# Four fused graph layers on Trainium2: the adjacency checks move to the input buffers, two chunks' operand pairs move to the last stage's buffers, and one subtraction moves from GpSimd to VectorE

## The chip, the cores and the metric

The kernel runs on one core of a Trainium2 chip. A core has a matrix engine (TensorE, "PE" in the profile), a vector engine (VectorE, "DVE"), a scalar engine (ScalarE, "ACT"), a general engine (GpSimd, "POOL") and a sync engine ("SP") that issues transfers between device memory (HBM) and the on-chip memory SBUF. PE writes its results into a second on-chip memory, PSUM. The metric is the device time of one execution in microseconds (us). A lower time is better. In the profile, "PEld" is PE loading the stationary operand of a matmul, and "PEclk" is the clock that PE was granted, as a share of full speed.

## The reference, cut to what matters

Four layers follow one another, each of the form x = x + layer(relu(layernorm(x))), on x of 8 batches x 2048 nodes x 64 features, with a 2048 x 2048 adjacency of zeros and ones. The change lies in the code of layers 2 and 3 only:

```python
# layer 2: three steps
v = causal_vars.at[:, intervention_idx].set(intervention_value)
for _ in range(3):
    effects = einsum('nm,bmd->bnd', adj, v)
    h = relu(einsum('bnk,dk->bnd', concatenate([v, effects], -1), W1) + b1)
    v = einsum('bnk,dk->bnd', h, W2) + b2
# layer 3: Chebyshev terms of the adjacency, then node-wise weights
w = einsum('nd,dkio->nkio', embedding, weight)          # d = 16, k = 3
x_g = stack([x, A @ x, 2 * A @ (A @ x) - x])            # over k
out = einsum('bnki,nkio->bno', x_g, w) + embedding @ bias
```

So for each batch there are five products with the adjacency: three in layer 2 and two in layer 3.

## The kernel before, in words

**Layout.** Two batches are handled as a pair p (of four): 2 x 64 features lie on the 128 partitions, the 2048 nodes along the free axis, in four chunks c of 512 columns. The transposed adjacency stays in SBUF as 16 tiles of 128 rows (`aT`, the last four named `aTl` in the profile).

**The product with the adjacency.** `spread` (L1459) adds up 16 row tiles into one PSUM tile `acc` per chunk. For precision each operand is two float32r tiles, `hi` (the rounded value) and `lo` (what the rounding left), so a chunk takes 32 matmuls. The operand pairs of the four chunks are made by `moved` (L1431), from matmuls with a small weight into PSUM (`py`), or by `turned` (L1448), from transposes. In `moved` with a bias, VectorE writes `yb` (L1443), ScalarE rounds it to `hi` (L1444) and GpSimd subtracts to get `lo` (L1445). In the other cases VectorE makes `lo` (L1440 and L1456).

**Stages of one pair.** `enter` (L1468) loads a chunk of the pair's input (`xp`), normalises it with `norm` (PE `mean`, DVE `xc`, ACT `q`, PE `var`, ACT, DVE `v`; L719 to L727) and makes the first operand pair. Then three steps follow, each over four chunks: step 0 and 1 make the next step's operands with `moved` (`yb` of chunk c belongs to the next step). Step 2 adds the input again (`xq`), writes the sum with a bias (`bq`) to device memory, normalises and makes operands with `turned`. Then one more product (`y1`), and the last stage: a product per chunk (`y2`), and for each of its four node tiles k a transpose (`px`), twelve matmuls `u` (L1541), products with the embedding (`pr`, L1549), their sums (L1553), a first addition into `fold` (L1559) and, on GpSimd, the rest (L1560 to L1562) and the store of `ot`. In the last stage of pair p the chunks of pair p+1 are entered; the last one, c = 3, after the loop, so that it meets the last tile's operations and the start of the next step 0.

**The checks.** The fused code holds only if the adjacency is zeros and ones. `check` (L1410) loads a 128 x 512 piece of it (`raw`, L1417, on SP's queue) and has VectorE compare it in place (L1419), with the number of offenders in a column of `bad`. There are 64 pieces. `check(2)` is called for every chunk of every step, so the first pair and the second take 24 checks each and the third 16. After everything, a flag made from `bad` decides on a slower general path, which this input doesn't take.

**Buffers and order.** A tile takes the next buffer of its tag in a pool; with n buffers it waits for the readers of the tile n earlier. Pool `f_in` has two buffers for tag "x" (`xp` of `enter`, `xq` of step 2, `xr` of the last stage). Pool `f_sb` has tags "hi" and "lo" with six buffers each, "fold" with two and "pr" with three (`pr` and `bq`). `raw` is in "fold". Each engine executes its own list of instructions in order, and SP issues its transfers in order. A scheduler sets these lists when the program is built; they can differ from the order of the source.

Of the kernel before, what the change touches and what calls it, by code (L numbers as in the profile page):

```python
# [8 lines left out]
FP = mybir.dt.float32  # L9
FR = mybir.dt.float32r  # L10
AF = mybir.ActivationFunctionType
OP = mybir.AluOpType
# [4 lines left out]
P = 128  # L17
# [4 lines left out]
CW = 512  # L22
# [5 lines left out]
def half(b2):  # L28
    return slice(b2 * 64, (b2 + 1) * 64)


def cols(c, w=CW):
    return slice(c * w, (c + 1) * w)
# [1353 lines left out]
def layers23(kit, aT, x2_dram, x3_dram, out):  # L1387

    tc, nc, t = kit.tc, kit.nc, kit.t
# [3 lines left out]
    W1v, W1e, W2, Wvc, Wec, cb = kit.W1v, kit.W1e, kit.W2, kit.Wvc, kit.Wec, kit.cb  # L1393
# [3 lines left out]
    fin = ctx.enter_context(tc.tile_pool(name="f_in", bufs=2, reuse_waits="tile"))  # L1397
    w2 = ctx.enter_context(tc.tile_pool(name="w2f", bufs=1, reuse_waits="tile"))
    sb = ctx.enter_context(tc.tile_pool(name="f_sb", bufs=2, reuse_waits="tile"))
    ps = ctx.enter_context(tc.tile_pool(name="f_ps", bufs=2, space=PSUM, reuse_waits="tile"))  # L1400

    def norm(dst, src):

        mean = ps.tile([P, CW], FP, tag="tp", name="mean")
        var = ps.tile([P, CW], FP, tag="tp", name="var")
        xc = fin.tile([P, CW], FP, tag="ca", name="xc")
        q = fin.tile([P, CW], FP, tag="q", name="q", bufs=1)
        kit.norm(dst, src, mean, var, xc, q)

    def check(n):  # L1410

        for _ in range(n):
            if not todo:
                return
            m, h = todo.pop(0)
            a = sb.tile([P, CW], FP, tag="fold", name="raw")
            nc.sync.dma_start(out=a, in_=t["adjT"][m * P : (m + 1) * P, cols(h)])  # L1417
            k = 7 + NCW * m + h
            nc.vector.scalar_tensor_tensor(  # L1419
                a, a, 0.5, a, op0=OP.is_gt, op1=OP.not_equal, accum_out=kit.bad[:, k : k + 1]  # L1420
            )

    todo = [(m, h) for m in range(NT) for h in range(NCW)]

    def parts():
        return (
            sb.tile([P, 4, P], FR, tag="hi", name="hi", bufs=6),
            sb.tile([P, 4, P], FR, tag="lo", name="lo", bufs=6),
        )

    def moved(v, c, W, bias):  # L1431

        py = ps.tile([P, 4, P], FP, tag="tp", name="py")
        for k in range(4):
            m = 4 * c + k
            mm(py[:, k, :], v[:, m * P : (m + 1) * P], W, start=True, stop=True)  # L1436
        hi, lo = parts()
        if bias is None:
            nc.scalar.copy(hi, py)
            nc.vector.tensor_tensor(lo, py, hi.bitcast(FP), op=OP.subtract)  # L1440
        else:
            yb = fin.tile([P, 4, P], FP, tag="ca", name="yb")
            nc.vector.tensor_tensor(yb, py, bias[:, None, :].to_broadcast([P, 4, P]), op=OP.add)  # L1443
            nc.scalar.copy(hi, yb)  # L1444
            nc.gpsimd.tensor_tensor(lo, yb, hi.bitcast(FP), op=OP.subtract)  # L1445
        return hi, lo

    def turned(v, c):  # L1448

        tp = ps.tile([P, 4, P], FP, tag="tp", name="tp")  # L1450
        for k in range(4):
            m = 4 * c + k
            nc.tensor.transpose(tp[:, k, :], v[:, m * P : (m + 1) * P], ident)
        hi, lo = parts()
        nc.scalar.copy(hi, tp)  # L1455
        nc.vector.tensor_tensor(lo, tp, hi.bitcast(FP), op=OP.subtract)  # L1456
        return hi, lo

    def spread(acc, y, c, start):  # L1459

        for m in range(NT):
            for part in y[m // 4]:
                mm(acc, part[:, m % 4, :], aT[m][:, cols(c)], start=start, stop=m == NT - 1 and part is y[m // 4][1])  # L1463
                start = False

    v = fin.tile([P, N], FP, name="v", bufs=1)
# [19 lines left out]
    for p in range(NP):  # L1486
        for step in range(3):
            yn = []
            for c in range(NCW):
                acc = ps.tile([P, CW], FP, tag="acc", name="acc")  # L1490
                check(2)
                mm(acc, Wvc if step else W1v, v[:, cols(c)], start=True, stop=False)  # L1492
                spread(acc, y, c, False)
                nc.scalar.activation(v[:, cols(c)], acc, AF.Relu, bias=b1c if step else b1)
                if step < 2:
                    yn.append(moved(v, c, Wec, cb))
                    continue
                pv = ps.tile([P, CW], FP, tag="tp", name="pv")
                mm(pv, W2, v[:, cols(c)], start=True, stop=True)
                xp = fin.tile([P, CW], FP, tag="x", name="xq")  # L1500
                nc.sync.dma_start(out=xp, in_=x2_dram[p, :, cols(c)])
                nc.vector.scalar_tensor_tensor(xp, pv, b2c, xp, op0=OP.add, op1=OP.add)
                bq = sb.tile([P, CW], FP, tag="pr", name="bq", bufs=3)
                nc.sync.dma_start(out=bq, in_=kit.bias_dram[:, cols(c)])
                nc.gpsimd.tensor_add(bq, bq, xp)
                nc.sync.dma_start(out=x3_dram[p, :, cols(c)], in_=bq)
                norm(v[:, cols(c)], xp)
                yn.append(turned(v, c))
            y = yn


        y1 = sb.tile([P, N], FP, tag="y1", name="y1", bufs=1)
        yn, after = [], []
        for c in range(NCW):
            acc = ps.tile([P, CW], FP, tag="acc", name="acc")
            spread(acc, y, c, True)
            nc.scalar.copy(y1[:, cols(c)], acc)
            yn.append(turned(y1, c))
        for c in range(NCW):
            acc = ps.tile([P, CW], FP, tag="acc", name="acc")  # L1520
            spread(acc, yn, c, True)
            y2 = fin.tile([P, CW], FP, tag="ca", name="y2")
            nc.scalar.copy(y2, acc)
            xp = fin.tile([P, CW], FP, tag="x", name="xr")
            nc.sync.dma_start(out=xp, in_=x3_dram[p, :, cols(c)])
            if c > 0 and p + 1 < NP:
                after.append(enter(p + 1, c - 1))
            for k in range(4):
                i = 4 * c + k
                ns, ks = slice(i * P, (i + 1) * P), slice(k * P, (k + 1) * P)  # L1530
                px = ps.tile([P, P], FP, tag="tp", name="px")
                nc.tensor.transpose(px, xp[:, ks], ident)
                xs = sb.tile([P, 2, F], FP, tag="xs", name="xs", bufs=1)
                nc.scalar.copy(xs.rearrange("p h f -> p (h f)"), px)
                pr = []
                for w in range(2):
                    u = [ps.tile([P, 8, F], FP, tag=f"u{h}", name=f"u{h}") for h in range(2)]
                    for kk, src in enumerate((v[:, ns], y1[:, ns], y2[:, ks])):
                        for h in range(2):

                            one = mm(  # L1541
                                u[h].rearrange("p d o -> p (d o)"), src[half(h), :], W3[half(h), kk, cols(w)],
                                start=kk == 0, stop=kk == 2,
                            )
                            if kk or h:
                                tc.keep_in_program_order(one)
                    for h in range(2):
                        a = sb.tile([P, 8, F], FP, tag="pr", name="pr", bufs=3)
                        nc.vector.tensor_tensor(  # L1549
                            a, u[h], emb[:, i, 8 * w : 8 * w + 8, None].to_broadcast([P, 8, F]), op=OP.mult  # L1550
                        )
                        if w:
                            nc.vector.tensor_add(pr[h], pr[h], a)  # L1553
                        else:
                            pr.append(a)
                fold = sb.tile([P, 2, 4, F], FP, tag="fold", name="fold")
                ot = sb.tile([P, 2, F], FP, tag="ot", name="ot", bufs=1)
                for h in range(2):
                    nc.vector.tensor_add(fold[:, h], pr[h][:, 0:4, :], pr[h][:, 4:8, :])  # L1559
                nc.gpsimd.tensor_add(fold[:, :, 0:2, :], fold[:, :, 0:2, :], fold[:, :, 2:4, :])  # L1560
                nc.gpsimd.tensor_add(ot, fold[:, :, 0, :], fold[:, :, 1, :])  # L1561
                nc.gpsimd.tensor_add(ot, ot, xs)  # L1562
                nc.sync.dma_start(
                    out=out[2 * p : 2 * p + 2, ns, :].rearrange("h p f -> p h f"), in_=ot
                )
        y = after + [enter(p + 1, NCW - 1)] if p + 1 < NP else None
# [102 lines left out]
```

## Time and profile before

| | |
|---|---|
| three runs | 2201.65, 2203.05, 2203.95 us; median 2203.05 us |
| the profiled execution | 2206.68 us, its span 2204.9 us |
| mean granted clock of PE | 0.98 |
| PE busy | 2091.0 us (95%), 9132 matmuls |
| VectorE busy | 1220.0 us (55%) |
| ScalarE busy | 450.4 us (20%) |
| GpSimd busy | 299.3 us (14%) |
| layers 2 and 3 | about 1014 us to the end, some 297 us per pair |
| in 1010 to 2205 us | PE busy 1161.0, VectorE 458.2, ScalarE 177.0, GpSimd 169.2 us |
| chain that ended last | PE 54%, issue 23%, DMA 7%, DVE 6%, POOL 5% of the span |

A line of the groups reads: source line, engine, operation, output <- inputs, their shapes and types, count, then busy time in us and mean ns of one, then the idle time of the engine just before such instructions and what ended it. A line of the timeline has its start in us, its duration, the instruction and, in brackets, the idle time before it and what ended that. A line of the waits has the waiting instruction, the instruction it waited for, the total in us, the number of waits and the longest. Busy times on PE are those of the records, whose ends are modelled and overlap; the pace is read from one start to the next. "PEld" overlaps PE.

### The profile page before, as it was taken

How to read it: one execution, taken by the hardware profiler on the slowest of the kernel's cores; microseconds unless marked ns; L12 is line 12 of the kernel's file. 1: busy time of each engine (PE TensorE's matmuls, PEld its weight loads, DVE VectorE, ACT ScalarE, POOL GpSimd, SP SyncE). 2: the span in 40 equal slices, each digit the busy share in tenths (PEclk: the TensorE clock that was granted, in tenths of full speed). 3: DMA queues.
4: the chain of work that ended last, by engine and by line, in shares of the span. 5: the costliest groups of instructions: out<-in, count | busy, mean ns of one | idle time of the engine just before them, and what ended most of it. 6: DMA issues, size and time to landing. Idle time of an engine off the chain costs nothing.

```text
span 2204.9 us, 23720 instructions
## 1 busy us (share of the span) xinstructions
PE 2091.0 (95%) x9132; PEld 1153.5 (52%) x9132; DVE 1220.0 (55%) x1890; ACT 450.4 (20%) x848; POOL 299.3 (14%) x416
## 2 busy tenths in 40 slices
PE   7999899886999999998999998999999999999997
PEld 4776656522222222224766546774457664576653
DVE  6675588866878787884213564115551235501265
ACT  4322244464110202002121101120111201112100
POOL 0211154401000000000110121101111011211022
PEclk9999899998999999999999999999999999999999
DMA  4665362156011111104210014000130100101000
GB/s 122 195 205 153 102 216 50 37 157 194 19 58 34 44 39 53 39 29 122 77 43 8 22 26 133 21 23 16 28 93 13 44 10 21 42 1 34 11 18 12
DMA packets 86443, 141.32 MB, mean 64 GB/s; under 512 B 33072, under 2 KB 33328, under 8 KB 84080
## 3 DMA queue, kind: packets, MB, share of 16 engines
q1 hardware_dynamic: 68272, 89.10, 13.7%
q0 software_dynamic: 18048, 50.60, 7.6%
q8 instruction: 74, 1.21, 0.2%
q14 instruction: 49, 0.40, 0.1%
HBM read 108.93 MB, written 30.74 MB: 63 GB/s over the span
## 4 chain that ended last, share of the span: by engine, by line
PE 54%; issue 23%; DMA 7%; DVE 6%; POOL 5%; ACT 2%; SPq 0%; POOLq 0%; DVEq 0%; ACTq 0%
PE acc L1463 16%; PE o L1332 11%; PE dn L1338 6%; PE u L1541 4%; DMA raw<-in_adjT 3%; PE acc L913 3%; PE pgs L1136 2%; PE var L724 2%; POOL fold L1560 2%; PE mean L719 2%; PE py L1436 1%; PE acc L1492 1%; DVE ex L1134 1%; POOL ot L1561 1%; POOL ot L1562 1%
## 5 line engine op out<-in xcount | busy, mean ns | idle before, releaser
L1463 PE MATMUL acc<-aT,hi 128*128 128x512 f32 x960 | 401.4, 418 | 0.0
L1463 PE MATMUL acc<-aT,lo 128*128 128x512 f32 x960 | 388.5, 405 | 0.0
L1332 PE MATMUL o<-pt,hS 128*64 128x512 f32 x1024 | 268.2, 606 | 4.3 <-DVE pt L1347 4.3
L1347 DVE SCALAR_TENSOR_TENSOR pt<-R,wd,aT 128x1024 f32<-128x1024 f32 x192 | 238.9, 1280 | 41.5 <-PE dn L1338 20.8
L1541 PE MATMUL u<-W3f,y 64*128 64x512 f32 x1024 | 258.2, 592 | 0.0
L1549 DVE TENSOR_TENSOR pr<-u,embf 128x512 f32<-128x512 f32 x256 | 171.3, 687 | 123.1 <-PE u L1541 111.0
L1463 PEld LDWEIGHTS acc<-aT,hi 128*128 128x128 f32 x960 | 180.9, 188 | 61.8 <-issue 23.2
L1463 PEld LDWEIGHTS acc<-aT,lo 128*128 128x128 f32 x960 | 180.9, 188 | 51.4 <-issue 13.6
L1541 PEld LDWEIGHTS u<-W3f,y 64*128 64x128 f32 x1024 | 104.1, 187 | 124.8 <-issue 124.8
L1332 PEld LDWEIGHTS o<-pt,hS 128*64 128x64 f32 x1024 | 70.5, 137 | 185.9 <-issue 178.7
L1541 PE MATMUL u<-W3f,v 64*128 64x512 f32 x512 | 146.4, 617 | 0.0
L1338 PE MATMUL dn<-pt,vd 128*32 128x512 f32 x1024 | 143.8, 600 | 0.5 <-DVE pt L1347 0.5
L913 PE MATMUL acc<-at,Y 128*128 128x512 f32 x512 | 139.2, 419 | 1.8 <-DVE ev L922 1.8
L1463 PE MATMUL acc<-aTl,lo 128*128 128x512 f32 x320 | 129.1, 404 | 5.5 <-DVE lo L1440 3.7
L1463 PE MATMUL acc<-aTl,hi 128*128 128x512 f32 x320 | 128.2, 401 | 6.0 <-ACT hi L1444 6.0
L1560 POOL TENSOR_TENSOR fold<-fold 128x256 f32<-128x256 f32 x64 | 47.6, 744 | 555.9 <-DVE fold L1559 555.9
L913 PEld LDWEIGHTS acc<-at,Y 128*128 128x128 f32 x512 | 97.5, 198 | 25.2 <-issue 3.4
L1443 DVE TENSOR_TENSOR yb<-py,cb_f 128x512 f32<-128x512 f32 x32 | 22.1, 690 | 158.4 <-PE py L1436 158.4
L721 ACT ACTIVATE q<-xc 128x512 f32<-128x512 f32 (+1 forms) x56 | 38.7, 691 | 262.7 <-DVE xc L720 256.0
L1553 DVE TENSOR_TENSOR pr<-pr 128x512 f32<-128x512 f32 x128 | 88.1, 688 | 2.2
L1419 DVE SCALAR_TENSOR_TENSOR raw<-raw 128x512 f32<-128x512 f32 x64 | 48.3, 760 | 72.5 <-DMA raw<-in_adjT 72.5
L1456 DVE TENSOR_TENSOR lo<-tp,hi 128x512 fp32r<-128x512 f32 x32 | 22.1, 692 | 117.5 <-ACT hi L1455 117.5
(275 smaller groups left out, 2694.9 us busy)
## 6 DMA issues: line engine op xcount, KB each, us to landing
at<-in_adjT POOLq DMA_DIRECT2D x32, 512.0 KB, 4.6
raw<-in_adjT SPq DMA_DIRECT2D x64, 256.0 KB, 3.3
aT<-in_adjT POOLq DMA_DIRECT2D x12, 1024.0 KB, 6.6
R<-r_dram SPq DMA_DIRECT2D x16, 512.0 KB, 3.6
hi_dram<-hi SPq DMA_DIRECT2D x16, 264.0 KB, 2.5
lo_dram<-lo SPq DMA_DIRECT2D x16, 264.0 KB, 3.4
hhi<-hi_dram POOLq DMA_DIRECT2D x16, 264.0 KB, 3.1
hlo<-lo_dram POOLq DMA_DIRECT2D x16, 264.0 KB, 3.2
```

What stands on the lines that cost most here:

```text
L719: mm(mean[:, cols(c)], self.avg, src[:, cols(c)], start=True, stop=True)
L724: mm(var[:, cols(c)], self.avg, q[:, cols(c)], start=True, stop=True)
L913: mm(acc[p], Y[h][:, m, p, :], at[:, k, :], start=m + h == 0, stop=m == NT - 1 and h == 1)
L1332: mm(o[half(b2), cols(k)], hS[:, m, half(b2)], pts[b2][:, cols(k)], start=m == 0, stop=m == NT - 1)
L1338: mm(dn[q : q + 32, :], vd[:, m, b2 : b2 + 1].to_broadcast([P, 32]), pts[b2][:, cols(k)], start=m == 0, stop=m == NT - 1, tile_position=(0 ...
L1347: nc.vector.scalar_tensor_tensor(pt, R[b2], wd[:, m, b2 : b2 + 1], aT[m][:, s].bitcast(FP), op0=OP.max, op1=OP.mult)
L1419: nc.vector.scalar_tensor_tensor(a, a, 0.5, a, op0=OP.is_gt, op1=OP.not_equal, accum_out=kit.bad[:, k : k + 1])
L1463: mm(acc, part[:, m % 4, :], aT[m][:, cols(c)], start=start, stop=m == NT - 1 and part is y[m // 4][1])
L1541: one = mm(u[h].rearrange("p d o -> p (d o)"), src[half(h), :], W3[half(h), kk, cols(w)], start=kk == 0, stop=kk == 2,)
L1549: nc.vector.tensor_tensor(a, u[h], emb[:, i, 8 * w : 8 * w + 8, None].to_broadcast([P, 8, F]), op=OP.mult)
L1553: nc.vector.tensor_add(pr[h], pr[h], a)
L1560: nc.gpsimd.tensor_add(fold[:, :, 0:2, :], fold[:, :, 0:2, :], fold[:, :, 2:4, :])
```

## The change

It has four parts, all in `layers23`. First, a check's tile `raw` takes a buffer of tag "x" in `f_in` and not of "fold" in `f_sb`. Second, `check(2)` is called in steps 0 and 1 only, so that each of the four pairs has 16 checks. Third, the operand pairs of chunks 2 and 3 that are made in steps 0 and 2 take their `hi` and `lo` from tags "fold" (chunk 2) and "pr" (chunk 3). Fourth, `lo` of `moved` with a bias is made on VectorE and not on GpSimd. In the changed file the lines up to L1425 keep their numbers and later ones stand 5 or 6 further on (L1443 to L1445 become L1448 to L1450).

```diff
     def check(n):
...
-            a = sb.tile([P, CW], FP, tag="fold", name="raw")
+            a = fin.tile([P, CW], FP, tag="x", name="raw")
             nc.sync.dma_start(out=a, in_=t["adjT"][m * P : (m + 1) * P, cols(h)])
...
-    def parts():
+    def parts(lent=None):
+
+        if lent:
+            return tuple(sb.tile([P, 4, P], FR, tag=lent[0], name=n, bufs=lent[1]) for n in ("hi", "lo"))
         return (
             sb.tile([P, 4, P], FR, tag="hi", name="hi", bufs=6),
             sb.tile([P, 4, P], FR, tag="lo", name="lo", bufs=6),
         )
 
-    def moved(v, c, W, bias):
+    LENT = (None, None, ("fold", 2), ("pr", 3))
+
+    def moved(v, c, W, bias, lent=None):
...
-        hi, lo = parts()
+        hi, lo = parts(lent)
...
             nc.scalar.copy(hi, yb)
-            nc.gpsimd.tensor_tensor(lo, yb, hi.bitcast(FP), op=OP.subtract)
+            nc.vector.tensor_tensor(lo, yb, hi.bitcast(FP), op=OP.subtract)
...
-    def turned(v, c):
+    def turned(v, c, lent=None):
...
-        hi, lo = parts()
+        hi, lo = parts(lent)
...
-                check(2)
+                if step < 2:
+                    check(2)
...
                 if step < 2:
-                    yn.append(moved(v, c, Wec, cb))
+                    yn.append(moved(v, c, Wec, cb, None if step else LENT[c]))
...
-                yn.append(turned(v, c))
+                yn.append(turned(v, c, LENT[c]))
```

## The prediction, made before the changed kernel ran

> **What bounds the kernel now.** I read the engine table first (PE busy 95% of the span), then the groups of the stretch from 1010 us on, which is layers 2 and 3, then PE's waits there, and then the stretches of time around the longest waits. PE is in its steady state throughout: one `acc` matmul per 0.233 us (32 in 7.46 us). So only what makes PE stand still can move the time. PE's waits from 1018 us on (engine, line, what it waited for: total us, times, longest):
>
> ```profile
> PE acc L1463 <- ACT hi L1444: 6.0, 2, 3.1
> ...
> PE acc L1463 <- DVE lo L1440: 3.7, 2, 2.2
> ...
> PE acc L1463 <- POOL lo L1445: 1.7, 2, 0.9
> ```
>
> These six waits all come from the checks. One, in batch pair 0 at 1070 us, in the timeline (start, duration, instruction, idle before it):
>
> ```profile
> 1066.60 0.69 DVE L1419 SCALAR_TENSOR_TENSOR raw<-raw 128x512 f32<-128x512 f32 x1 [2.85 <-DMA raw<-in_adjT]
> ...
> 1070.78 0.69 DVE L1419 SCALAR_TENSOR_TENSOR raw<-raw 128x512 f32<-128x512 f32 x1 [2.51 <-DMA raw<-in_adjT]
> ...
> 1071.39 0.69 DVE L1443 TENSOR_TENSOR yb<-py,cb_f 128x512 f32<-128x512 f32 x1
> ...
> 1072.79 0.49 PE L1463 MATMUL acc<-aTl,hi 128*128 128x512 f32 x1 [3.13 <-ACT hi L1444]
> 1074.13 0.80 PE L1463 MATMUL acc<-aTl,lo 128*128 128x512 f32 x1 [0.86 <-POOL lo L1445]
> ```
>
> VectorE (DVE) stands in front of checks whose loads have not landed; `yb`, ready to run since about 1064, stands behind them, then hi, then lo, then PE. Matmul starts show what it takes: 1069.26 to 1072.79 is 3.53, less one pace 0.23, 3.3 us; 1072.79 to 1074.13 is 1.1 us more. Then the clock (window, us, PE, PEld, DVE, ACT, POOL busy, PEclk, DMA share, GB/s):
>
> ```profile
> 1074.00:1077.50 3.50, 3.37 (x8) 2.70 (x9) 1.40 (x4) 0.00 (x0) 0.08 (x1) 0.51 0.37 119
> 1374.40:1377.90 3.50, 3.50 (x9) 2.22 (x7) 1.12 (x5) 0.69 (x1) 0.00 (x0) 0.51 0.23 75
> 1633.80:1637.20 3.40, 3.40 (x10) 2.62 (x9) 0.99 (x3) 0.65 (x1) 0.00 (x0) 0.50 0.48 134
> ```
>
> For 3.41 us after each such stop PE runs at half clock, 0.43 us a matmul: 3.41 x (1 - 0.233/0.43) = 1.56 us lost. What all this costs per batch pair is seen by comparing the same work, from the last `mean` of the entry to the end of step 1 or so, in pairs 1 (24 checks), 2 (16) and 3 (none left):
>
> ```profile
> 1320.28:1414.90 94.62, 88.84 (x384) 66.44 (x383) 29.45 (x65) 13.20 (x21) 13.02 (x11) 0.98 0.27 80
> 1620.04:1711.00 90.96, 88.33 (x384) 66.68 (x383) 22.39 (x50) 13.27 (x21) 12.91 (x11) 0.98 0.20 60
> 1916.22:2003.50 87.28, 86.80 (x385) 65.66 (x384) 10.86 (x17) 13.28 (x21) 11.99 (x11) 1.00 0.05 14
> ```
>
> So checks cost pair 1 7.3 us and pair 2 3.7 us; pair 0, by its own stop, 3.3 + 1.1 + 1.56 = 6.0. All checks together: about 17 us of 2203. That is the most that the change can touch.
>
> **What the skill says.** "TensorE: Matmul & The Clock Gate", What's actually happening: half clock comes after an idle window of about 3.4 us, full clock after a busy one, and the windows run free; the traces' 0.51 for 3.41 us agrees. "Perfetto Trace Analysis", Tensor Engine Instruction: VectorE, ScalarE and GpSimd execute strictly in order; `yb` above agrees. "GPSIMD Engine Reference", 3.1 Elementwise: GpSimd takes 1.96 times VectorE's time for an addition of two tensors; here 1.27 against 0.69 us, 1.85 times.
>
> **The change by parts.** *lo on VectorE.* 32 instructions leave GpSimd and come to VectorE:
>
> ```profile
> L1445 POOL TENSOR_TENSOR lo<-yb,hi 128x512 fp32r<-128x512 f32 x32 | 42.3, 1321 | 297.4 <-ACT hi L1444 264.0 <-DMA raw<-in_adjT 33.4
> L1419 DVE SCALAR_TENSOR_TENSOR raw<-raw 128x512 f32<-128x512 f32 x64 | 48.3, 760 | 72.5 <-DMA raw<-in_adjT 72.5
> ```
>
> 42 us off GpSimd, 32 x 0.69 = 22 us onto VectorE, hidden by PE's 300 us per pair. It matters only where PE waits for lo: about 0.6 us at each of the two stops of pairs 0 and 1; without that cover lo would stand behind checks, as L1440 does.
>
> *Lent buffers.* Chunks 2 and 3 of steps 0 and 2 take "fold" and "pr" instead of the six "hi"/"lo" buffers. In step 0 these are free early (GpSimd's last fold of the pair before). In step 2 chunk 3 follows the write-outs of `bq` in the same three "pr" buffers, which land by 1145 us in pair 0 while the part is needed at 1160: 15 us in hand. In return no hi waits for `acc` matmuls five chunks back, which held ScalarE but never PE. Cost 0; without the cover up to a few us per pair.
>
> *Checks: 16 in each pair, none in step 2.* Pairs 0 and 1 have 8 fewer each, pair 3 has 16 where it had none. The stop of step 0 in pairs 0 and 1 goes: two input buffers take a pair of loads per 4.07 us (check to check of one buffer, e.g. 1049.87, 1053.93, 1058.00), so the 16 checks of pair 0, the pairs of loads from 1032 on, end near 1064, when chunk 3's yb is ready, and its lo is done by 1066.3, needed at 1069.5; in pair 1 they end near 1357 (chunk 3's py: 1369). Removed: 6.0 in pair 0, and in pair 1 3.0 + 1.1 + 1.56 = 5.7. Sum -11.7. SP issues the loads of xq and bq only behind all 16 checks (about 1064), needed at 1116: nothing. At the entry of pair 0 check 2's load waits for `xc` (1031.6), lands 3.5 us later and runs just ahead of `v` (1035.46 today): +0.4, inside the margin of the sum.
>
> *Checks in the input buffers ("x"): a new wait.* This is the part that decides. At each passage from pair to pair the instruction order of the changed kernel on VectorE is: check 1, the two first products of the last tile, check 2, check 3, the remaining six operations of the tile and `xc` of the entry's last chunk, checks 4 and 5, `v`, check 6, lo. Today no check stands before `xc`:
>
> ```profile
> 1315.13 0.42 SPq L1501 DMA_DIRECT2D xq<-xd  x1
> ...
> 1320.38 0.69 DVE L1549 TENSOR_TENSOR pr<-u,embf 128x512 f32<-128x512 f32 x1 [0.81 <-PE u L1541]
> ...
> 1323.44 0.68 DVE L720 TENSOR_TENSOR xc<-xp,mean 128x512 f32<-128x512 f32 x1
> ...
> 1324.84 1.13 PE L724 MATMUL var<-q,avg_f 128*128 128x512 f32 x2 [0.48 <-ACT q L721]
> ...
> 1327.39 0.69 DVE L727 SCALAR_TENSOR_TENSOR v<-xc,q 128x512 f32<-128x512 f32 x1 [2.16 <-ACT q L726]
> 1328.14 1.16 PE L1436 MATMUL py<-W1e_f,v 128*128 128x128 f32 x8
> ```
>
> One of the two "x" buffers holds that entry's xp until `xc` has read it, and `xc` stands behind check 3. So checks 1 to 3 all go through the other buffer, each load waiting for the check before. Check 1's load goes out where the freed buffer is filled today, 1315.13; with 3.3 us to landing (median of the 64 loads) it runs at 1318.45; check 2 4.07 later, 1322.5; check 3 1326.6, over at 1327.2. The product of 1320.38 runs at 1327.2: +6.85; `xc` and PE's `var` with it. PE executes in order and everything behind `var` waits: it stands from about 1324.4 to 1331.7. Check 5, whose load can go only after `xc` (1331.0), puts `v` at 1335.0, +7.57. The stop is longer than a whole clock window, so half clock follows for 3.41 to 6.8 us, a loss of 1.56 to 3.1, I take 2.3: with var at +6.85, 0.28 us of slack before py today used up, py comes 6.85 - 0.28 + 2.3 = +8.9 (lowest +8.1, highest +9.7).
>
> Three passages: 3 x 8.9 = +26.7. They replace the waits for lo L1440 that the same passages have now: 1.75 at 1331, and 2.31 + 1.5 (half clock) at 1631; the third has none. Net 26.7 - 5.6 = +21.1.
>
> Sum: +21.1 - 11.7 = **+9.4 us**. The profiled execution took 2206.68 us (span 2204.9), 3.6 above the median 2203.05; the difference goes onto the median: **2212.5 us**, in its own trace a span of about 2214. From the ends above, +8.1 or +9.7 a passage, and 1.5 either way on the gain, this case has 2208.5 to 2216.5.
>
> **Rivals.** *Passages cost half* (loads land faster, or the half clock stays out): +4.5 a passage less 5.6, less 11.7: -3.8, 2199; with the chain of three cut only to two, +5 to +6: around 2203. For it: nothing in the trace; landing spreads from 2.9 to 9.0 with 3.3 in the middle, so shorter loads save 3 x 0.4 at most. *Faster: the passage is hidden altogether.* Then all of the 17 us go: 2186. It decides if check 3 ends before 1320.4, 6.8 us earlier than I find; the net is zero at a passage of 5.8 us. Against it: the loads can't overlap in one buffer. *The gain fails too*: if loads in step 0 land like the slow ones (9.0 us, while the DMA share is 0.85 up to 1032), the last checks still stand ahead of chunk 3's yb: -11.7 shrinks to 0 and the time is 2224. *Lent buffers stall*: hi of step 2's chunk 3 waits for a write-out behind late loads; 15 us are in hand, four pairs of 1 to 2 us plus 1.5 of clock: 2222. *Nothing moves*, because both sides cancel or the parts were all under cover: 2203.
>
> **Numbers.** Forecast 0.66; half-cost passages 0.11 (half of that within 0.2%); hidden 0.04; gain fails 0.11; lent buffers 0.05; nothing 0.03. A measurement of this kernel can tell about 0.2%, 4.4 us. The upper edge takes the failing gain partly in, the lower the half-cost passages: 2204 to 2221.5. Slower by over 0.2% 0.84, within 0.2% 0.10, faster 0.06.
>
> **What would show it.** Right: PE waits `var <- q` of about 7 us, three times, ending near 1326, 1627 and 1928 in the new trace (today's 1324.8, 1624.6 and 1920.8, moved by the terms above), half clock behind each; DVE checks with 3 us of idle waiting for `raw` ahead of the last tile's products; waits of acc for hi and for lo of moved gone; the window of pair 3 some 9 us longer than 87.3. Wrong: no such `var` wait, or a wait of acc for hi in step 0 still there, or one for a lent buffer in step 2.

## The result and the profile after

The changed kernel takes 2221.43 us (median of six runs, 2218.37 to 2224.54) where the kernel before takes 2202.38 (six runs, 2201.3 to 2203.95): ratio 1.0086, 95% interval 1.0073 to 1.0099, so it is 19.1 us slower (by the interval, 16 to 22). Forecast was 2212.5 us, +9.4, with a range of 2204 to 2221.5: the measured median lies inside it by 0.07 us. The profiled execution took 2219.91 us with a span of 2217.8, 12.9 more than the span before.

PE's waits from 1018 us on, in the changed kernel (what was waited for: total us, times, longest us), are all of these:

```profile
PE var L724 <- ACT q L721: 26.5, 13, 7.9
PE pbad L1629 <- DVE pr L1555: 2.7, 1, 2.7
PE py L1441 <- DVE v L727: 2.1, 7, 0.6
PE py L1441 <- DVE v L1479: 1.3, 3, 0.4
```

The three kinds of waits of `acc` that the prediction showed (6.0, 3.7 and 1.7 us) are gone, and `var` now waits 26.5 us. Before, its line was:

```profile
PE var L724 <- ACT q L721: 5.3, 13, 0.5
```

The timeline of the first passage from pair to pair in the changed kernel (start, duration, instruction, idle before it) shows how. It begins with check 1:

```profile
1313.12 0.75 DVE L1419 SCALAR_TENSOR_TENSOR raw<-raw 128x512 f32<-128x512 f32 x1 [0.60 <-DMA raw<-in_adjT]
...
1313.90 0.35 SPq L1417 DMA_DIRECT2D raw<-in_adjT  x1
...
1317.23 0.69 DVE L1419 SCALAR_TENSOR_TENSOR raw<-raw 128x512 f32<-128x512 f32 x1 [2.15 <-DMA raw<-in_adjT]
...
1321.04 0.69 DVE L1419 SCALAR_TENSOR_TENSOR raw<-raw 128x512 f32<-128x512 f32 x1 [3.11 <-DMA raw<-in_adjT]
...
1321.66 0.69 DVE L1555 TENSOR_TENSOR pr<-u,embf 128x512 f32<-128x512 f32 x1
...
1324.72 0.68 DVE L720 TENSOR_TENSOR xc<-xp,mean 128x512 f32<-128x512 f32 x1
...
1326.12 2.08 PE L724 MATMUL var<-q,avg_f 128*128 128x512 f32 x2 [7.38 <-ACT q L721]
...
1331.54 1.05 PE L1441 MATMUL py<-W1e_f,v 128*128 128x128 f32 x8
```

The load for check 2 goes out only when check 1 is done, at 1313.90. Checks 1 to 3 follow each other at 4.1 and 3.8 us through one buffer, and ahead of checks 2 and 3 VectorE sits idle for their loads. The last tile's third product comes only behind check 3, then `xc`, then `var`, with PE standing for 7.4 us. The clock behind the three waits (window, us, PE, PEld, DVE, ACT, POOL busy, PEclk, DMA share, GB/s):

```profile
1323.84:1330.67 6.83, 4.55 (x9) 2.94 (x10) 4.26 (x11) 1.95 (x3) 2.01 (x3) 0.50 0.37 100
1624.21:1631.04 6.83, 3.62 (x7) 2.21 (x8) 4.16 (x11) 1.95 (x3) 2.01 (x3) 0.50 0.43 122
1924.59:1934.83 10.24, 6.15 (x13) 4.16 (x14) 6.17 (x14) 1.95 (x3) 2.01 (x3) 0.50 0.37 113
```

Half clock holds for two or three windows of 3.41 us, the first of which begins while PE still stands. In step 0 of pair 0 the last chunk's `yb` no longer stands behind checks (0.88 us of idle, waiting for its own matmuls):

```profile
1064.26 0.69 DVE L1448 TENSOR_TENSOR yb<-py,cb_f 128x512 f32<-128x512 f32 x1 [0.88 <-PE py L1441]
```

The stretch from the entry's last `mean` to the first `mean` of step 2 holds everything of a pair that moves between these two traces; here all four pairs of the changed kernel, same columns:

```profile
1029.56:1112.51 82.95, 82.95 (x366) 61.92 (x365) 25.75 (x55) 14.23 (x22) 0.13 (x1) 1.00 0.21 64
1314.42:1413.72 99.30, 91.92 (x394) 68.46 (x392) 27.62 (x58) 13.96 (x22) 2.44 (x5) 0.97 0.19 55
1615.60:1714.58 98.98, 91.48 (x393) 68.13 (x392) 27.60 (x58) 13.95 (x22) 2.43 (x5) 0.97 0.18 55
1916.45:2017.00 100.55, 92.64 (x394) 68.97 (x393) 27.81 (x59) 13.95 (x22) 2.44 (x5) 0.95 0.18 54
```

Before, the same four stretches were:

```profile
1029.50:1118.27 88.77, 84.76 (x366) 62.90 (x365) 27.00 (x63) 14.17 (x22) 10.43 (x9) 0.98 0.24 74
1320.28:1418.04 97.76, 91.98 (x393) 68.03 (x392) 30.20 (x66) 13.89 (x22) 13.16 (x12) 0.98 0.27 77
1620.04:1714.21 94.17, 91.54 (x393) 68.30 (x392) 23.14 (x51) 13.96 (x22) 13.04 (x12) 0.98 0.19 58
1916.22:2006.57 90.35, 89.87 (x394) 67.19 (x392) 11.61 (x18) 13.97 (x22) 12.14 (x12) 1.00 0.05 14
```

What lies between them (step 2 and layer 3) took 202.0 us in every pair before and 201.9 after. The account of layers 2 and 3 in these traces is therefore 82.95 + 99.30 + 98.98 + 100.55 - (88.77 + 97.76 + 94.17 + 90.35) = +10.7 us. A further 2.2 us lie after the last output was computed, which is taken up below.

### The profile page after: what moved, and what is told of

The parts are those of the page before. It is cut to its first block, busy times and chain, and to the rows that moved or that the text cites. A ratio compares the mean times of both kernels' runs of the same rounds, so it can differ in the third digit from the quotient of the medians.

```text
span 2217.8 us, 23631 instructions
## 1 busy us (share of the span) xinstructions
PE 2094.3 (94%) x9132; PEld 1156.4 (52%) x9132; DVE 1237.3 (56%) x1922; ACT 450.1 (20%) x848; POOL 257.5 (12%) x384
## 4 chain that ended last, share of the span: by engine, by line
PE 62%; issue 19%; DVE 5%; POOL 5%; DMA 5%; ACT 2%; POOLq 0%; SPq 0%; DVEq 0%; ACTq 0%
PE acc L1468 23%; PE o L1332 11%; PE dn L1338 6%; PE acc L913 3%; PE var L724 2%; PE u L1547 2%; PE py L1441 2%; PE pgs L1136 2%; POOL fold L1566 2%; PE acc L1498 2%; PE mean L719 2%; DMA raw<-in_adjT 1%; POOL ot L1567 1%; POOL ot L1568 1%; DVE ex L1134 1%
## 5 line engine op out<-in xcount | busy, mean ns | idle before, releaser
L1468 PE MATMUL acc<-aT,hi 128*128 128x512 f32 x960 | 406.3, 423 | 0.0
L1448 DVE TENSOR_TENSOR yb<-py,cb_f 128x512 f32<-128x512 f32 x32 | 22.1, 690 | 152.5 <-PE py L1441 152.5
L724 PE MATMUL var<-q,avg_f 128*128 128x512 f32 x128 | 73.3, 664 | 31.9 <-ACT q L721 31.9
```

The source lines that it names most:

```text
L724: mm(var[:, cols(c)], self.avg, q[:, cols(c)], start=True, stop=True)
```

## The experiments

All were timed beside the kernel before on the same chip; differences are between medians, ratios with their 95% interval. The table has the four stretches (us, from the starts of the `mean` instructions) of all traces; it is what the experiments are read by, since whole executions scatter more than the stretches do.

| kernel | pair 0 | pair 1 | pair 2 | pair 3 |
|---|---|---|---|---|
| before, first trace | 88.77 | 97.76 | 94.17 | 90.35 |
| before, second trace | 87.98 | 98.64 | 92.40 | 90.39 |
| full change, first trace | 82.95 | 99.30 | 98.98 | 100.55 |
| full change, second trace | 82.90 | 99.87 | 99.24 | 99.03 |
| 16 checks per pair alone | 83.05 | 94.25 | 94.02 | 92.65 |
| raw in "x" alone | 83.43 | 99.14 | 99.24 | 90.37 |
| raw in "x" and 16 checks | 82.96 | 99.43 | 99.02 | 98.72 |
| full change, no lent buffers | 82.88 | 99.18 | 98.73 | 98.68 |
| full change, lo on GpSimd | 82.89 | 99.81 | 99.39 | 98.73 |
| full change, no checks at all | 82.79 | 90.37 | 90.40 | 90.37 |
| full change, raw in four quarters of y1 | 83.59 | 92.06 | 91.63 | 91.92 |
| full change, raw in two quarters of y1 | 82.75 | 91.77 | 92.17 | 91.46 |
| raw in y1 and 16 checks, nothing else | 83.09 | 94.52 | 92.64 | 93.24 |

**Theories.** "Passages": the chain of checks in the "x" buffers, ahead of `xc`, costs about 9 us at each of three passages, the stops of step 0 are worth about 12, and lent buffers and `lo` on VectorE nothing. Rivals: lent buffers or `lo` on VectorE carry the part of the 19 us that the forecast lacks; or checks on VectorE cost the same wherever they stand.

**Sixteen checks per pair alone.**

```diff
-                check(2)
+                if step < 2:
+                    check(2)
```

> The kernel before with one part of the change: 16 checks per pair (none in step 2), raw still in the fold buffers. Theory 'passages' (the chain of checks in the x buffers ahead of xc costs +8 to +10 us at each of three passages, the stops of step 0 in pairs 0 and 1 are worth -11.7, the other parts nothing): the stops of step 0 go, the third passage gets what the second has (+3.8), so about -8 us, 2194 to 2196; no wait of var over 1 us. Rival 'fewer checks do not free step 0' (the stop comes from the pace of the loads, not their number): 0 to +4 us, with the wait of acc for hi at 1070 us still there.

Measured 2197.41 against 2205.94 us, -8.5 (ratio 0.9925, 0.9897 to 0.9954). The stops of step 0 are gone, and the passages keep the wait for lo, behind checks, now in all three:

```profile
PE acc L1463 <- DVE lo L1440: 6.3, 4, 2.1
PE var L724 <- ACT q L721: 4.9, 12, 0.5
```

The number of checks caused the stops of step 0 in the fold buffers, and this one part of the change, alone, is a gain of the size that was forecast for it.

**Raw in the "x" buffers alone**, with 24, 24, 16 and 0 checks.

```diff
-            a = sb.tile([P, CW], FP, tag="fold", name="raw")
+            a = fin.tile([P, CW], FP, tag="x", name="raw")
```

> The kernel before with raw in the x buffers and nothing else (24, 24, 16 and no checks in the four pairs). 'Passages': waits of var of 7 us at the first and second passage, none at the third, where no check is left; the stops of step 0 stay or come back in part because 24 checks reach to chunk 3; +8 to +14 us in all, of which the two passages +12. Rival 'the chain needs 16 checks in every pair': no waits of 7 us, 0 to +3 us.

Measured 2213.22 against 2206.21 us, +7.0 (1.0029, 1.0012 to 1.0046). Its stretches of pairs 1, 2 and 3:

```profile
1325.66:1424.80 99.14, 91.55 (x394) 68.19 (x393) 25.37 (x58) 13.96 (x22) 13.25 (x13) 0.97 0.22 66
1628.99:1728.23 99.24, 91.76 (x393) 68.47 (x392) 22.45 (x51) 13.96 (x22) 13.78 (x13) 0.97 0.18 55
1930.21:2020.58 90.37, 89.89 (x393) 67.19 (x392) 11.61 (x18) 13.95 (x22) 12.12 (x12) 1.00 0.05 14
```

Two passages of 99 us, and a third of 90.4 where pair 3 has no checks: this part alone makes the passage, and the second part carries it into pair 3. Two things were expected wrongly. The time is 1 us below the range of +8 to +14, and the stops of step 0 did not come back with 24 checks (pair 0 takes 83.4 us). The later checks go on into step 2 there, and the parts between the stretches took 203.1 and 204.2 us in pairs 0 and 1 and not 202.0.

**Raw in "x" and 16 checks**, that is the first two parts without the others.

> The kernel before with two parts: raw in the x buffers and 16 checks per pair; no lent buffers, lo still on GpSimd. 'Passages': three waits of var of 7 to 8 us and the same time as the full change within 3 us, so +16 to +22 us. Rival 'lent buffers or lo on VectorE carry the part of the +19 us that was not forecast': +9 us only, since the other 10 come from the parts left out here.

Measured 2215.88 against 2205.94 us, +9.9 (1.0038, 1.0024 to 1.0052). The time is not within 3 us of the full change's, and alone it would suit the rival. The trace does not: it has the three waits of `var`, and its stretches are those of the full change within 0.2 us in pairs 1 and 2.

```profile
PE var L724 <- ACT q L721: 25.8, 12, 7.5
```

**The full change without lent buffers.**

```diff
-    LENT = (None, None, ("fold", 2), ("pr", 3))
+    LENT = (None, None, None, None)
```

> The full change without the lent buffers (all parts in the six hi and lo buffers again). 'Passages': the same as the full change within 3 us, +16 to +22 us. Rival 'lent buffers stall': up to 9 us faster than the full change, near +10 us.

Measured 2215.67 against 2205.94 us, +9.7 (1.0043, 1.0026 to 1.006). Again the time is the rival's, and again the stretches are those of the full change (99.18, 98.73, 98.68): within the stretches of the full change the lent buffers are worth nothing, either way.

**The full change with lo on GpSimd.**

```diff
-            nc.vector.tensor_tensor(lo, yb, hi.bitcast(FP), op=OP.subtract)
+            nc.gpsimd.tensor_tensor(lo, yb, hi.bitcast(FP), op=OP.subtract)
```

> The full change with the second parts of moved on GpSimd again. 'Passages': the same as the full change within 3 us (three waits of var of 7 to 8 us, no wait of acc in step 0), stretches of 99 to 100.5 us. Rival 'GpSimd beside the checks slows them': checks of up to 1.7 us, stretches of 101 us and more in pairs 1 to 3.

Measured 2220.01 against 2206.65 us, +13.4 (1.0072, 1.0052 to 1.0092), with the stretches of the full change and no wait of `acc`. A check of 1.49 us occurs beside GpSimd's work, somewhat as the rival said, but no wait of PE is added by it.

**The full change again, unaltered.**

> The changed kernel, unaltered, timed again beside the kernel before, since its first measurement (+19 us) and its first trace (+10.6 us in layers 2 and 3 against the first trace of before) differ. 'The trace is right, the rest is the spread of executions': +9 to +14 us. 'The first measurement is right and the first trace a lucky one': +17 to +21 us, with half-clock stretches of 10.2 us and more behind the three waits of var.

Measured 2220.84 against 2206.21 us, +14.6 (1.0062, 1.0038 to 1.0086), just above the first theory's range; the two measurements' intervals overlap from 1.0073 to 1.0086. The second trace has the same stretches within 1.6 us.

**The kernel before again, unaltered.**

> The kernel before, unaltered, for a second trace. If executions differ mainly in layers 0 and 1 by the phase of the half-clock stretches, the time to the entry of layer 2 moves by up to some us from 1029.5 and the stretches of layers 2 and 3 repeat within 1.6 us each (88.8, 97.8, 94.2, 90.4).

Layer 2's entry came at 1030.4 us and the stretches at 87.98, 98.64, 92.40 and 90.39, within 1.8 us of the first trace (the largest difference, in pair 2, is a half-clock stretch that is not there). Over all 13 traces, whose layers 0 and 1 are the same, the entry's last `mean` comes between 1023.1 us (64.9 us of half clock before it) and 1039.2 us (99.0 us of half clock).

**The full change without any check.**

```diff
         for _ in range(n):
-            if not todo:
-                return
+            return
```

> The changed kernel without any check: the 64 loads of raw and their comparisons are left out, so bad stays zero and the input is not checked. 'Passages': this is what the change would give with its checks for nothing: layers 2 and 3 shorter by 17 us than before, 2185 to 2187 us where before has 2203; each stretch from the entry's last mean to step 2 takes 90.4 us as pair 3 of before. Rival 'lent buffers or lo on VectorE cost something by themselves': the stretches stay above 91 us.

Measured 2187.99 against 2206.21 us, -18.2 (0.992, 0.9895 to 0.9945). The four stretches add up to 17.1 us less than in the first trace of before, where the prediction had put all checks at about 17. Those of pairs 1 to 3:

```profile
1314.09:1404.46 90.37, 89.89 (x394) 67.19 (x392) 17.14 (x26) 13.96 (x22) 1.77 (x4) 1.00 0.05 14
1606.32:1696.72 90.40, 89.92 (x394) 67.22 (x393) 17.14 (x26) 13.95 (x22) 1.77 (x4) 1.00 0.05 14
1898.62:1988.99 90.37, 89.89 (x393) 67.19 (x392) 17.14 (x26) 13.96 (x22) 1.77 (x4) 1.00 0.05 14
```

So 90.4 us is the stretch with nothing in the way, `lo` on VectorE and lent buffers included, and a passage of the full change costs the mean of its six stretches less this: 99.5 - 90.4 = 9.1 us.

**Raw in the quarters of y1.** The buffer of `y1` (8 KB per partition) is free from the last tile's matmuls to the fourth product of the next pair. A check takes one quarter of it, so that no check can be loaded before PE has read `y1` for the last tile, and `xc` comes ahead of all of them.

```diff
+    raws = [None]
     for p in range(NP):
+        raws[0] = sb.tile([P, N], FP, tag="y1", name="raw", bufs=1)
...
-            a = fin.tile([P, CW], FP, tag="x", name="raw")
+            a = raws[0][:, cols((len(todo)) % 4)]
```

> The full change with raw neither in x nor in fold, but in the four quarters of the y1 buffer, which lies free from the last tile of one pair to the fourth product of the next: four loads under way at once, and the first can go only when PE has read y1 for the last tile, so that xc stands ahead of all checks. 'Passages': the three waits of var vanish (0.7 us as before), step 0 stays free of stops, and most of the 17 us that checks cost in the kernel before is saved: 2186 to 2191 us, -12 to -17. Rival 'checks on VectorE cost wherever they stand' (v or lo is held up instead): -5 to +5 us.

Measured 2194.05 against 2205.94 us, -11.9 (0.9921, 0.9893 to 0.9948): at the edge of what was expected, and faster than both kernels. The waits of `var` are back to 5.3 us, the longest 0.5, and 1.2 to 1.7 us per passage remain, as short waits for `v` and for lo behind checks.

**Two quarters of y1**, and not four (`% 2` in the line above).

> The full change with raw in two quarters of the y1 buffer and not in four: as many check buffers as the x tag offers, but with xc ahead of the first check and never more than two checks ahead of v. 'The place of the checks, not the number of buffers, makes the passage': no wait of var over 1 us, stretches of 91 to 93.5 us, -9 to -16 us. Rival 'two buffers are too few': lo or yb is held up behind the 4 us pace, stretches of 94 to 97 us, -5 to +5 us.

Measured 2194.58 against 2206.65 us, -12.1 (0.9935, 0.9907 to 0.9963). Waits and stretches of pairs 1 to 3:

```profile
PE var L724 <- ACT q L721: 5.3, 13, 0.5
PE acc L1468 <- DVE lo L1445: 3.3, 3, 1.6
```

```profile
1315.26:1407.03 91.77, 90.12 (x393) 67.09 (x392) 28.24 (x58) 13.96 (x22) 2.61 (x4) 1.00 0.20 59
1608.88:1701.05 92.17, 90.12 (x394) 67.09 (x392) 28.16 (x58) 13.96 (x22) 2.66 (x4) 1.00 0.19 59
1903.25:1994.71 91.46, 90.11 (x393) 67.10 (x392) 28.73 (x59) 13.96 (x22) 2.44 (x4) 1.00 0.20 59
```

With two check buffers, as many as "x" has, the passage is gone, so it was not their number that made it. What differs is where they lie. One "x" buffer is freed before the last tile is through, the other is held by the xp that `xc` has to read, and VectorE has checks 1 to 3 ahead of `xc`. In `y1` two loads are under way at once (issued at 1315.72 and 1316.19), and `xc` (1318.42) comes ahead of the first check (1319.46). How much of the gain belongs to the order and how much to the second load under way was not separated: raw in "x" with `xc` ahead of the checks was not tried.

**Raw in y1 and 16 checks, without lent buffers and with lo on GpSimd.**

> The kernel before with 16 checks per pair and raw in the quarters of the y1 buffer; lo stays on GpSimd and no buffers are lent. If the lent buffers and lo on VectorE are worth nothing by themselves, the same as the version with both within 3 us: -10 to -16 us against before, each stretch from the entry's last mean to step 2 at 91 to 92.5 us. If one of them is needed to keep step 0 free of stops, a wait of acc for hi or lo of 1 to 4 us comes back there and the stretches take 93 to 96 us.

Measured 2193.66 against 2206.65 us, -13.0 (0.9947, 0.9929 to 0.9964). The time is that of the two versions above, as the first case had it. The trace is nearer to the second: PE waits for lo at all three passages (1.9, 1.4 and 2.0 us), and the stretches are 94.5, 92.6 and 93.2 us against 91.5 to 92.2, some 4.9 us more in all.

```profile
PE acc L1463 <- DVE lo L1440: 5.6, 4, 1.9
```

They are as long as those of 16 checks alone, with raw in "fold" (94.3, 94.0 and 92.7). So in these traces, one of each version, the place in `y1` shortens the stretches only together with the other two parts, which seem worth 1.6 us per pair there. Which of the two it is was not tried.

## Why the prediction was right, and where it was short

The direction and the mechanism were right: three new waits of `var` outweigh the stops that go. The size of the total was not: +9.4 us was forecast, the stretches of the traces moved by +11.2, and the first measurement gave +19.1, twice the forecast. That its median lies inside the range, by 0.07 us, is luck. The upper edge had been drawn out for another case, the failing gain, and that case did not occur.

**The stops of step 0** went, in both traces and in every experiment with 16 checks. Pair 0: forecast -6.0, in the traces -5.8 (88.77 to 82.95) and -5.1 (87.98 to 82.90). The steps held: 16 checks are over before the last chunk's `yb`.

**The passage** is the step on which the forecast rested, and it held by place and by size. Forecast was `var` 6.85 us late and py 8.9 us late. In the first passage `var` starts at 1326.12 and py at 1331.54. Against before (1324.84 and 1328.14, where the pair starts 5.86 us later) that is 7.1 and 9.3 us. Over six passages the cost is 9.1. The three `var` waits end at 1326.1, 1627.4 and 1928.7 (forecast 1326, 1627, 1928). Two things could delay py: check 5, behind which `v` stands (the check ran until 1329.4, `v` from 1329.6 to 1330.3), and the half clock. The half clock decides, as in the prediction's sum: py starts right behind PE's own matmuls, 1.2 us after `v` is done. As to pairs: pair 1 was forecast at 8.9 - 1.75 - 5.7 = +1.5, and the means of two traces each differ by +1.4; pair 2 at +5.1, measured +5.8; pair 3 at +8.9, measured +9.4.

**Lent buffers and lo on VectorE** were put at nothing, and leaving either out of the full change leaves the stretches as they are. So the rival of lent buffers that stall falls, though its 2222 us lie nearest to the measured time. So does "the gain fails too", at 2224 us: no trace of the full change has a stop in step 0. Here the time alone would have named the wrong case. (The 1.27 us that the prediction gives for GpSimd's subtraction is the shortest of the 32; its own line has a mean of 1.32, which is 1.9 times VectorE's time. Nothing rests on it.)

**What is short.** The sum was +9.4; the means of the two traces each give -5.5 + 1.4 + 5.8 + 9.4 = +11.2 us in the stretches. Three terms were a little off, and one was missing:

- Three passages at 9.1 us and not 8.9 make +0.6. The waits of before in pairs 1 and 2, at the passages and in step 0 together, were worth 10.7 us in its two traces (98.2 and 93.3 less 90.4 each) and not 11.3, another +0.5, and the stop of pair 0 was worth 0.5 less. The half clock was sized well: between the start of `var` and the return of full clock PE ran for 3.6 to 6.2 us, 4.8 in the mean of six, and 4.8 x (1 - 0.233/0.43) is 2.2 us lost, where 2.3 was taken.
- The end has no term in the sum. GpSimd's last operation, in the kernel before (L1562) and in the changed kernel (L1568):

```profile
2198.36 0.45 POOL L1562 TENSOR_TENSOR ot<-ot,xs 128x128 f32<-128x128 f32 x1
...
2209.05 0.45 POOL L1568 TENSOR_TENSOR ot<-ot,xs 128x128 f32<-128x128 f32 x1
```

From its end to the end of the span it is 6.1 us before and 8.3 after, 8.8 in the second trace of the full change. In the change without lent buffers it is 6.4, and it is near 6 in the other experiments. So some 2.5 us of the loss belong to the full change's way out of the program: GpSimd's closing instruction (DRAIN) starts 5.1 and 5.6 us after that last operation, in all other traces 2.8 to 3.1. Its cause is not shown. Lent buffers and lo on VectorE are not enough for it, since the versions with raw in `y1` have both and end in about 6 us.

Together the traces account for 11.2 + 2.5 = 13.7 us, and for 14.0 with what lies outside the span, which is 2.1 to 2.2 us in all twelve timed executions of the full change and 1.8 to 1.9 in those of before. The repeated measurement (+14.6, interval 1.0038 to 1.0086) agrees with that. The first (+19.1, interval from +16.1) does not quite. The changed kernel itself took the same time in both, 2221.43 and 2220.84 us. It is the kernel before that differs: its first six runs have a median of 2202.38 us, and those beside the experiments, on three chips, 2205.94 to 2206.65. Why the first six were faster stays open. The experiments without lent buffers, or with the first two parts alone, came out at +9.7 and +9.9, near the forecast. Of the 5 us between them and +14.6 the end explains 2.8, and the rest is inside the intervals.

## What to carry to other kernels

A scratch tile that moves into another tag takes over that tag's life: ask when its buffers come free and who else holds one, because a load that can start earlier can also put its reader earlier in an engine's list, as it did here, and what is urgent then stands behind it. A job whose result nobody is waiting for is better tied to a buffer that comes free only after the urgent work. `y1` does that here: in the full change the same 16 checks in the same number of buffers cost 9.1 us per passage in "x" and 1.1 to 1.8 in two quarters of `y1`. And with several parts in one change, the stretches of the trace told apart what the total time, with its scatter of more than half a per cent, could not.

## What was not expected of the hardware

The same kernel scatters more than its first three runs said: they spread over 2.3 us, but 40 runs beside the first experiments lay between 2193.6 and 2219.2 us. Part of it lies before layer 2, where the 13 traces have the same work: its entry came between 1023 and 1039 us, with 65 to 99 us of half clock before it, and later where there is more of it in most traces but not all. In each trace every start and end of half clock, but for the end that the span cuts off, lies within 0.01 us of a multiple of 3.413 us from the first one, through the whole execution. The first half clock began at 29.55 us in one trace of before and at 27.12 in the other, which is not a whole number of such steps: the grid does not start with the kernel.

The half clock behind a wait also varies. The 17 waits of PE of 7.2 to 7.9 us at the passages, in all traces that have them, were followed by 6.8 or 10.2 us of half clock, counted from within the wait. The kernel before had eight waits of 1.6 to 3.1 us in its two traces: three of up to 1.8 us were followed by none, four by 3.4 us and one by 6.8. So a wait shorter than the "idle window of about 3.4 us" that the prediction speaks of was enough: with 16 checks alone, one of 1.9 us was followed by half clock, and one of 2.0 us was not.
